# LayerNorm's scaling of 48 tiles on GpSimd in place of ScalarE, in a fused cross-attention kernel

## The chip, the cores and the metric

The kernel runs on one core of one Trainium2 chip. A core has a matrix engine (TensorE, PE in the profile, with PEld for its weight loads), a vector engine (VectorE, DVE), a scalar engine (ScalarE, ACT), GpSimd (POOL), and SyncE (SP), which here only issues DMAs. Each engine executes its own instructions in the order in which the program lists them, and waits for other engines by semaphores. The metric is device time in microseconds (us) of one execution.

## The reference

The layer is cross-attention with a residual and a LayerNorm: x is (4, 2048, 512), the context is (4, 77, 512), there are 16 heads of 32 columns, and a mask hides part of the 77 context rows.

```python
qs  = (q @ wq) ; ks_ = (k @ wk) ; vs = (v @ wv)          # split into 16 heads of 32
scores = einsum('bhqd,bhkd->bhqk', qs, ks_) / sqrt(32)
scores = where(mask, -inf, scores)
attn = einsum('bhqk,bhkd->bhqd', softmax(scores), vs)     # heads joined again
out  = attn @ wo + q
mu   = mean(out) ; var = mean((out - mu) ** 2)            # over the 512 columns
return (out - mu) / sqrt(var + 1e-5) * gamma + beta
```

The change concerns the last line alone.

## The kernel before, in words

The 8192 rows of x are cut into 64 tiles of 128 rows. Two tiles make a pair (32 pairs), four tiles share one transposed load of x. Every product that needs it is split into a high part and a low remainder, so three matmuls stand for one.

The whole order of the work is written out by hand in a table of words, ORDER (lines 49 to 143). The kernel walks through it and calls one small function per word; since each engine executes in program order, the table sets the order on every engine. A word is a letter and a number, which is a tile, a pair or a group. The words that matter here:

- Q (PE) and q (DVE): the query projection, and its copy out of PSUM. i (ACT, line 265) and j (POOL, line 269): the high part and the remainder of the transposed x, 128x1024 each.
- S (PE, line 399): the scores of a tile. T (DVE, line 416): mask added and row maxima, four heads at a time. e (ACT, line 431): the exponentials, four heads at a time, with their sums. r (DVE, line 441): reciprocals of the sums. n (POOL, line 446): the tile's weights times these reciprocals, 128x1232.
- t (DVE, line 467): transpose of the weights. P (issued by SP mostly, line 478): twelve DMAs per pair that regroup them. V (PE, line 492): product with the values. a (ACT, line 521) and b (DVE, line 525): high part and remainder of its result.
- x (SP, line 533): a tile of x is loaded as the residual. O (PE, line 548): the output projection. + (DVE, line 557): the residual is added, which gives the tile o, 128x512.
- s (DVE, lines 568 and 569): mean and variance of the tile. v (POOL, lines 574 to 577): once per pair, the inverse root of variance plus epsilon, and minus the mean times that root. k (ACT, line 583): the tile times the root, plus the shift, in one pass over 128x512. f (POOL, lines 587 and 588): times gamma, then plus beta. w (SP, line 591): the tile is stored.

Tiles 48 to 63 go another way (letters u, y and z: DVE does the passes) and contain none of k, f and v. The tile o has eight buffers, the pair's mean and variance (mv) and its root (rn) three each. SP issues all loads, stores and most of the regrouping DMAs from one queue, in the table's order.

Of the kernel before, what the change touches and what calls it, by code (L numbers as in the profile page):

```python
# [8 lines left out]
F32 = mybir.dt.float32  # L9
# [3 lines left out]
AF = mybir.ActivationFunctionType  # L13
ALU = mybir.AluOpType
# [3 lines left out]
P = 128  # L18
# [31 lines left out]
R1 R0 R3 E l0 l2 C2 C0 C1 C3 g5 M4.4 A0 M0.1 M12.4 A1 M1.3 A3 M8.4 K2 A2 H2 J3 p i3 g4 J1 K0 i2 S0 I2 j2 S1 T0.1  # L50
e0.1 T0.2 H0 T0.0 j3 e0.0 T1.0 T0.3 e0.2 T1.1 Q4 T1.2 e0.3 F0 T1.3 I0 e1.2 r0 n0 S2 q4 e1.0 S3 T2.3 T2.0 Q7 i5 T2.1
e1.3 F2 j5 T2.2 t0 e1.1 Q6 i4 F1 g7 r1 Y1 e2.0 F3 L1 n1 T3.2 Q5 x1 T3.1 e2.1 q6 T3.3 e3.3 j4 t1 B0 e3.2 T3.0 P0.4s
q7 x2 e2.3 q5 P0.7s S4 D0 P0.5s e3.0 S6 P0.10s T4.3 P0.0s G0 B2 e3.1 R2 T4.0 g6 P0.2s e4.3 r3 P0.8s G3 n3 P0.11s B1
e2.2 D2 P0.6s T4.1 T4.2 e4.1 G2 r2 Q8 i7 t3 x11 n2 P0.3s e4.2 P0.9s T6.0 P0.1s T6.2 e4.0 j7 x0 Q9 T6.3 Z13.s t2
e6.0 Z0.s G1 e6.3 S5 r4 P1.0s T6.1 n4 P1.7s q8 Q10 e6.2 T5.3 P1.6s T5.0 P1.10s e6.1 T5.2 P1.3s T5.1 P1.5s i6 S7 t4
P1.1s Z1.s e5.3 Q11 j6 P1.11s T7.2 P1.9s e7.2 T7.3 Z2.s q9 P1.8s r6 e7.3 D1 Q13 n6 P1.4s T7.0 P1.2s T7.1 e7.0 g9
q10 x3 e7.1 Z12.s V0 q13 g8 q11 Z11.s a0.0 r7 e5.0 t6 V1 Z10.s n7 Z7.s e5.1 b0.0 S9 N t7 a1.1 Q12 e5.2 b1.1 P3.9s
a1.0 P3.5s r5 T9.0 n5 P3.11s e9.0 Q14 b1.0 P3.3s T9.2 Z8.s e9.2 T9.1 P3.2s T9.3 P3.4s e9.3 t5 Y0 S8 P3.10s a0.1 O2
P3.7s q12 i9 T8.1 P3.0s T8.0 e9.1 P2.3s T8.3 P3.8s q14 Z9.s e8.0 O3 T8.2 P3.1s b0.1 P3.6s e8.3 +2 Z5.s r9 P2.0s n9
e8.2 S10 +3 P2.7s S11 P2.2s T10.0 e8.1 s2 P2.9s O1 j9 s3 T10.3 e10.3 r8 T10.1 v1 g10 Q15 +1 e10.1 Z4.s t9 n8 P2.6s  # L60
k2 x6 T10.2 P2.11s e10.0 V3 f2 t8 i8 T11.3 P4.11s O0 e11.3 T11.2 P2.4s j8 q15 P4.9s a3.0 T11.0 P2.8s k3 T11.1 P2.1s
a3.1 S12 w2 e10.2 M16.4 P2.5s b3.1 Q19 +0 P4.6s e11.1 r10 P4.5s T12.2 n10 P2.10s b3.0 e11.2 T12.0 P4.10s O6 s0
P4.7s i10 f3 P4.8s s1 P4.0s e11.0 q19 T12.3 S13 e12.2 t10 v0 w3 V2 P4.3s r11 x7 T13.2 a2.0 n11 e13.2 P4.1s T13.1 O7
Z6.s +6 P4.4s T12.1 a2.1 k1 b2.0 P4.2s b2.1 e12.0 Z3.s f1 t11 O4 x4 x5 e12.3 g11 s6 P5.5s e12.1 j10 T13.3 P5.0s O5
# [20 lines left out]
P12.5s k18 S28 +20 P12.9s i17 V11 T28.1 g18 e28.1 T28.2 P12.10s j17 T28.0 P12.11s S29 s20 e28.2 P12.0s P12.6s t26
Q33 v10 P12.4s a11.1 e27.1 P12.2s f18 b11.1 P12.3s T29.0 a11.0 T28.3 Q32 e28.3 P12.8s r27 T29.2 x24 n27 b11.0 e28.0
T29.1 q33 O23 k20 T29.3 e29.0 M32.4 q32 r28 t27 k21 O22 i18 f21 +23 P13.10s e29.3 s23 x27 w18 e29.2 S30 +22 n28 w21
P13.5s V12 T30.1 e30.1 P13.9s T30.0 P13.6s T30.2 j18 a12.0 S31 x26 s22 e30.2 P13.2s T30.3 Q34 P13.3s t28 e29.1
P13.1s v11 P13.4s a12.1 T31.0 P13.7s f20 e30.3 T31.3 Q35 P13.11s T31.2 g19 e31.3 r29 P13.8s b12.1 P13.0s b12.0 n29
k23 q34 O25 T31.1 e30.0 f23 t29 e31.2 O24 +25 e31.0 P14.4s s25 x29 w20 k22 r30 q35 n30 P14.2s i19 S32 g20 +24  # L90
P14.7s V13 T32.1 e32.1 P14.10s j19 T32.2 P14.9s T32.0 e32.2 w23 S33 s24 P14.11s t30 Q37 P14.3s a13.1 v12 e31.1 x28
P14.5s T32.3 f22 b13.1 a13.0 P14.6s e32.3 T33.0 Q36 P14.1s r31 T33.2 P14.8s e32.0 q37 n31 P14.0s b13.0 x31 T33.1
e33.0 O27 T33.3 M36.4 k25 t31 k24 f25 e33.3 O26 q36 P15.1s r32 P15.6s +27 i20 w22 s27 n32 w25 e33.2 P15.10s S34 +26
e33.1 V14 x30 T34.1 j20 P15.11s T34.0 a14.0 P15.2s T34.2 e34.1 S35 P15.4s s26 P15.8s t32 Q38 v13 e34.2 P15.5s g21
# [10 lines left out]
t39 k32 f33 O34 i24 +35 s35 e41.3 q44 n40 w33 e41.2 P19.10s S42 +34 P19.5s V18 T42.1 e42.1 P19.9s j24 T42.0 x38
T42.2 P19.2s a18.0 S43 s34 e42.2 P19.3s t40 P19.6s Q46 v17 e41.1 P19.8s P19.1s T42.3 f32 P19.4s T43.0 a18.1 e42.3
P19.7s T43.3 Q47 P19.0s T43.2 e43.3 g25 r41 b18.1 n41 P19.11s b18.0 x41 q46 k35 O37 T43.1 e42.0 f35 t41 e43.2 q47
P20.7s O36 r42 w32 +37 e43.0 n42 P20.1s s37 L3 k34 w35 i25 P20.5s S44 +36 P20.9s j25 V19 T44.1 e44.1 P20.10s T44.2
P20.11s T44.0 P20.4s e44.2 S45 s36 P20.6s t42 g26 Q49 v18 a19.1 P20.8s e43.1 P20.2s f34 b19.1 P20.3s T45.0 a19.0
# [64 lines left out]
def xattn_layernorm(  # L174
# [404 lines left out]
    def scale(t):  # L579
        o = od[t]  # L580
        tt = t % 2
        rn = rns[t // 2]
        nc.scalar.activation(o, o, AF.Identity, bias=rn[:, 1, tt : tt + 1], scale=rn[:, 0, tt : tt + 1])  # L583
# [176 lines left out]
```

## Time and profile before

| What | Value |
|---|---|
| median of 3 runs | 526.71 us (525.96 to 527.35) |
| span of the profiled execution, first to last instruction | 525.7 us |
| PE busy | 507.2 us, 96% |
| DVE busy | 476.0 us, 91% |
| ACT busy | 460.4 us, 88% |
| POOL busy | 405.5 us, 77% |
| k on ACT (line 583) | 48 passes, 37.9 us busy, 807 ns each |
| f on POOL (lines 587, 588) | 48 and 48 passes, 62.5 and 62.4 us busy, 1302 and 1300 ns each |
| n on POOL (line 446) | 63 whole tiles, 142.8 us busy, 2267 ns each |
| granted PE clock | 0.997 of full speed |

The profiled execution's own time beside its span is not listed apart: the profile gives the span alone, and the three runs give times of whole executions, whose median lies 1.0 us above it.

A busy share is an average over the span. The chain of waits follows the last instruction back, at each step to what released it or to the instruction before it on its engine. A group's row gives busy time, the mean duration of one, the engine's idle time just before, and who ended that idle time.

### The profile page before, as it was taken

How to read it: one execution, taken by the hardware profiler on the slowest of the kernel's cores; microseconds unless marked ns; L12 is line 12 of the kernel's file. 1: busy time of each engine (PE TensorE's matmuls, PEld its weight loads, DVE VectorE, ACT ScalarE, POOL GpSimd, SP SyncE). 2: the span in 40 equal slices, each digit the busy share in tenths (PEclk: the TensorE clock that was granted, in tenths of full speed). 3: DMA queues.
4: the chain of work that ended last, by engine and by line, in shares of the span. 5: the costliest groups of instructions: out<-in, count | busy, mean ns of one | idle time of the engine just before them, and what ended most of it. 6: DMA issues, size and time to landing. Idle time of an engine off the chain costs nothing.

```text
span 525.7 us, 20274 instructions
## 1 busy us (share of the span) xinstructions
PE 507.2 (96%) x6845; PEld 388.8 (74%) x6845; DVE 476.0 (91%) x2572; ACT 460.4 (88%) x2215; POOL 405.5 (77%) x371
## 2 busy tenths in 40 slices
PE   9999999999989999999999999999999999999994
PEld 6987777778767777777777777767777777767662
DVE  5798988989979989998989989998998999999997
ACT  6699999998989999999999999999999999987400
POOL 2475736889889889969989887988888689869551
PEclk9999999999999999999999999999999999999998
DMA  8948577785797677988887687797868987388555
GB/s 300 401 125 241 148 205 196 195 236 147 205 243 226 189 197 225 217 219 219 215 225 207 178 224 226 184 254 195 213 190 225 259 251 189 91 219 218 158 176 199
DMA packets 59261, 110.85 MB, mean 211 GB/s; under 512 B 9430, under 2 KB 11758, under 8 KB 59158
## 3 DMA queue, kind: packets, MB, share of 16 engines
q1 hardware_dynamic: 55702, 102.75, 69.1%
q0 software_dynamic: 2496, 5.77, 3.9%
q10 hardware_dynamic: 960, 1.05, 0.8%
q8 instruction: 54, 0.88, 0.7%
q14 instruction: 49, 0.40, 0.3%
HBM read 41.79 MB, written 16.78 MB: 111 GB/s over the span
## 4 chain that ended last, share of the span: by engine, by line
PE 51%; DVE 12%; DMA 10%; POOL 9%; SPq 9%; ACT 5%; issue 3%; POOLq 0%; DVEq 0%
PE pq L275 20%; PE po L548 15%; PE sc L399 7%; SPq L478 6%; PE pa L492 6%; DMA PT<-B 6%; ACT pbuf L431 4%; POOL o L587 3%; DVE B L467 3%; POOL o L588 2%; POOL pbuf L446 2%; DVE pbuf L416 2%; PE pv L326 2%; DMA stage_a<-xT 1%; POOL xtl L269 1%
## 5 line engine op out<-in xcount | busy, mean ns | idle before, releaser
L431 ACT ACTIVATE pbuf<-pbuf,nm 128x77 f32<-128x77 f32 x1024 | 352.7, 350 | 16.2 <-DVE nm L416 13.4
L431 ACT ACTIVATION_READ_ACCUMULATOR pbuf<-pbuf,nm 128x1 f32 x1024 | 194.6, 190 | 0.0
L416 DVE CUSTOM_DVE_ANT_0 pbuf<-sc,mb 128x77 f32<-128x77 f32 x1024 | 170.2, 231 | 9.6 <-PE sc L399 8.5
L446 POOL TENSOR_TENSOR pbuf<-pbuf,ri 128x1232 f32<-128x1232 f32 x63 | 142.8, 2267 | 39.4 <-DVE ri L441 23.6
L467 DVE STREAM_TRANSPOSE B<-pbuf 128x1280 f32<-128x1280 f32 x64 | 96.1, 1502 | 9.8 <-POOL pbuf L446 5.4
L548 PE MATMUL po<-woh,AH 128*128 128x512 f32 x256 | 102.6, 401 | 0.0
L548 PE MATMUL po<-woh,AL 128*128 128x512 f32 x256 | 100.1, 391 | 2.3 <-DVE AL L525 2.3
L275 PE MATMUL pq<-xth,wqh 128*128 128x512 f32 (+1 forms) x256 | 101.8, 398 | 0.2
L548 PE MATMUL po<-wol,AH 128*128 128x512 f32 x256 | 99.8, 390 | 0.0
L275 PE MATMUL pq<-xtl,wqh 128*128 128x512 f32 (+1 forms) x256 | 98.3, 384 | 0.0
L275 PE MATMUL pq<-xth,wql 128*128 128x512 f32 (+1 forms) x256 | 98.1, 383 | 0.0
L416 DVE DVE_READ_ACCUMULATOR2_ANT nm<- 128x1 f32 x1024 | 83.9, 82 | 0.0
L399 PEld LDWEIGHTS sc<-kct,q 32*64 32x64 f32 x4096 | 52.8, 130 | 32.9 <-issue 17.1
L587 POOL TENSOR_TENSOR o<-o,gam 128x512 f32<-128x512 f32 x48 | 62.5, 1302 | 13.7 <-ACT o L583 13.4
L269 POOL TENSOR_TENSOR xtl<-xtf,xth 128x1024 fp32r<-128x1024 f32 x28 | 67.3, 2403 | 6.7 <-ACT xth L265 6.6
L399 PE MATMUL sc<-kct,q 32*64 32x77 f32 x4096 | 63.6, 238 | 8.4 <-issue 3.8
L588 POOL TENSOR_TENSOR o<-o,bet 128x512 f32<-128x512 f32 x48 | 62.4, 1300 | 3.8
L492 PE MATMUL pa<-PT,vsb 96*32 96x256 f32 x992 | 59.9, 382 | 0.0
L521 ACT CAST AH<-pa 128x512 fp32r<-128x512 f32 x64 | 36.4, 572 | 25.0 <-DVE st L596 10.6
L548 PEld LDWEIGHTS po<-woh,AL 128*128 128x128 f32 x256 | 48.0, 188 | 13.8 <-DVE AL L525 3.5
L548 PEld LDWEIGHTS po<-woh,AH 128*128 128x128 f32 x256 | 48.0, 188 | 13.7 <-issue 2.0
L275 PEld LDWEIGHTS pq<-xth,wqh 128*128 128x128 f32 x256 | 48.1, 188 | 12.0 <-PE sc L399 0.5
(108 smaller groups left out, 666.0 us busy)
## 6 DMA issues: line engine op xcount, KB each, us to landing
PT<-B SPq DMA_DIRECT2D x343, 128.0 KB
xtf<-xT SPq DMA_DIRECT2D x28, 512.0 KB
o<-x SPq DMA_DIRECT2D x56, 256.0 KB
out<-o SPq DMA_DIRECT2D x56, 256.0 KB
PT<-B POOLq DMA_DIRECT2D x25, 128.0 KB, 3.8
xtf<-xT SPq DMA_DIRECT2D x4, 256.0 KB
stage_a<-wq SPq DMA_DIRECT2D x4, 256.0 KB
stage_a<-wk SPq DMA_DIRECT2D x4, 256.0 KB
```

The lines of the kernel that those rows point to most:

```text
L269: nc.gpsimd.tensor_tensor(l[:, c : c + 2], fx.pop((g, c)), xh[g][:, c : c + 2].bitcast(F32), ALU.subtract)
L275: nc.tensor.matmul(pq, w[:, c, m * P : (m + 1) * P], r[g][:, c, rs], start=(n == 0), stop=(n == 11))
L399: mm = nc.tensor.matmul(sc[j][r0 : r0 + SR, g * NK : (g + 1) * NK], qs[q, g, rs.start + r0 : rs.start + r0 + SR], kct[q, g, t // TPB, keys ...
L416: nc.vector.tensor_tensor_reduce(pb[:, h // 2, (h % 2) * NK : (h % 2 + 1) * NK], scs[t][j][:, g * NK : (g + 1) * NK], mb[:, t % TPB, keys_ ...
L431: nc.scalar.activation(pb[:, h // 2, (h % 2) * NK : (h % 2 + 1) * NK], pb[:, h // 2, (h % 2) * NK : (h % 2 + 1) * NK], AF.Exp, bias=nmax[t ...
L446: nc.gpsimd.tensor_tensor(pv, pv, rv.to_broadcast((P, NP, 2, NK)), ALU.mult)
L467: nc.vector.transpose(bt.rearrange("p c q r -> p q c r"), pbuf[t % NPB].rearrange("p q (c r) -> p q c r", c=5),)
L492: nc.tensor.matmul(pas[b, g // 2][HD * j : HD * (j + 1), (g % 2) * BLK : (g % 2 + 1) * BLK], vsb[:, 2 * b // TPB, h % 2, HD * (h // 2) : H ...
L521: nc.scalar.copy(*at_part(once(ahs, b, [P, NG, BLK], F32R, "AH"), b, i, by_tile))
L548: nc.tensor.matmul(pos[t], a[:, c, rs], w[:, c, :], start=(first and c == 0 and n == 0), stop=(c == NC_D - 1 and n == 2),)
L587: nc.gpsimd.tensor_tensor(o, o, gam, ALU.mult)
L588: nc.gpsimd.tensor_tensor(o, o, bet, ALU.add)
```

## The change

The words k0 to k47 are taken out of ORDER; the other words keep their order. What k did becomes the first of three passes in f: POOL subtracts the mean and multiplies by the root in one tensor_scalar instruction over 128x512, in place, with the two numbers of each row read from mv and rn. Since the mean is used as it is, v no longer makes the product of mean and root and its negative, and keeps two of its four operations on 128x2.

```diff
     def rsqrt(b):
-        rn = rns[b] = buf([P, 2, 2], F32, "rn", name=f"rn_{b}")
-        mv = mvs[b]
-        nc.gpsimd.tensor_tensor(rn[:, 0, :], mv[:, :, 1], eps, ALU.add)
-        nc.gpsimd.tensor_tensor(rn[:, 0, :], rn[:, 0, :], mhalf, ALU.pow)
-        nc.gpsimd.tensor_tensor(rn[:, 1, :], mv[:, :, 0], rn[:, 0, :], ALU.mult)
-        nc.gpsimd.tensor_tensor(rn[:, 1, :], rn[:, 1, :], mneg, ALU.mult)
-
-    def scale(t):
-        o = od[t]
-        tt = t % 2
-        rn = rns[t // 2]
-        nc.scalar.activation(o, o, AF.Identity, bias=rn[:, 1, tt : tt + 1], scale=rn[:, 0, tt : tt + 1])
+        rn = rns[b] = buf([P, 2], F32, "rn", name=f"rn_{b}")
+        nc.gpsimd.tensor_tensor(rn, mvs[b][:, :, 1], eps, ALU.add)
+        nc.gpsimd.tensor_tensor(rn, rn, mhalf, ALU.pow)
 
     def affine(t):
-        o = od[t]
+        o, tt = od[t], t % 2
+        mean, rstd = mvs[t // 2][:, tt, 0:1], rns[t // 2][:, tt : tt + 1]
+        nc.gpsimd.tensor_scalar(o, o, mean, rstd, ALU.subtract, ALU.mult)
         nc.gpsimd.tensor_tensor(o, o, gam, ALU.mult)
         nc.gpsimd.tensor_tensor(o, o, bet, ALU.add)
...
-        "v": lambda k, part: rsqrt(k), "k": lambda k, part: scale(k), "f": lambda k, part: affine(k),
+        "v": lambda k, part: rsqrt(k), "f": lambda k, part: affine(k),
```

The order of POOL's instructions in the middle of the program, before, from the split of x for group 9 to the normalise of tile 30 (o_20 and o_23 are tiles of the output, rn_11 the roots of pair 11, ri_29 the reciprocals of tile 29; the last figure of each name only numbers the buffers):

```order
L269 TENSOR_TENSOR xtl_9_4324<-xtf_9_0_4037,xth_9_4224 128x1024
L574 TENSOR_TENSOR rn_11_4399<-mv_11_4237,small_78 128x2
L575 TENSOR_TENSOR rn_11_4399<-rn_11_4399,small_78 128x2
L576 TENSOR_TENSOR rn_11_4399<-mv_11_4237,rn_11_4399 128x2
L577 TENSOR_TENSOR rn_11_4399<-rn_11_4399,small_78 128x2
L587 TENSOR_TENSOR o_20_3657<-o_20_3657,gam_76 128x512
L588 TENSOR_TENSOR o_20_3657<-o_20_3657,bet_77 128x512
L446 TENSOR_TENSOR pbuf2_82<-pbuf2_82,ri_29_4447 128x8x154
L587 TENSOR_TENSOR o_23_3617<-o_23_3617,gam_76 128x512
L588 TENSOR_TENSOR o_23_3617<-o_23_3617,bet_77 128x512
L446 TENSOR_TENSOR pbuf0_80<-pbuf0_80,ri_30_4513 128x8x154
```

The same place on POOL now (line numbers have shifted: 442 is the normalise, 575 the new pass):

```order
L265 TENSOR_TENSOR xtl_9_4301<-xtf_9_0_4016,xth_9_4200 128x1024
L569 TENSOR_TENSOR rn_11_4376<-mv_11_4214,small_78 128x2
L570 TENSOR_TENSOR rn_11_4376<-rn_11_4376,small_78 128x2
L575 TENSOR_SCALAR o_20_3639<-o_20_3639,mv_10_3943,rn_10_4094 128x512
L576 TENSOR_TENSOR o_20_3639<-o_20_3639,gam_76 128x512
L577 TENSOR_TENSOR o_20_3639<-o_20_3639,bet_77 128x512
L442 TENSOR_TENSOR pbuf2_82<-pbuf2_82,ri_29_4423 128x8x154
L575 TENSOR_SCALAR o_23_3599<-o_23_3599,mv_11_4214,rn_11_4376 128x512
L576 TENSOR_TENSOR o_23_3599<-o_23_3599,gam_76 128x512
L577 TENSOR_TENSOR o_23_3599<-o_23_3599,bet_77 128x512
L442 TENSOR_TENSOR pbuf0_80<-pbuf0_80,ri_30_4488 128x8x154
```

Two small operations on rn have gone, and a pass over 128x512 stands ahead of each multiplication by gamma, between two normalises.

The order of ACT's instructions around the scaling of tiles 20 and 21, before (line 431 are exponentials, x8 means eight in a row, line 583 is the scaling, line 265 the high part of x):

```order
L431 ACTIVATE pbuf1_81,sum_28_4039<-pbuf1_81,nm_28_4032 128x77 x8
L583 ACTIVATE o_20_3657<-o_20_3657,rn_10_4115 128x512
L431 ACTIVATE pbuf2_82,sum_29_4199<-pbuf2_82,nm_29_4133 128x77 x4
L583 ACTIVATE o_21_3409<-o_21_3409,rn_10_4115 128x512
L265 CAST xth_9_4224<-xtf_9_0_4037 128x1024
L431 ACTIVATE pbuf2_82,sum_29_4199<-pbuf2_82,nm_29_4133 128x77 x8
```

And now:

```order
L427 ACTIVATE pbuf1_81,sum_28_4018<-pbuf1_81,nm_28_4011 128x77 x8
L427 ACTIVATE pbuf2_82,sum_29_4176<-pbuf2_82,nm_29_4111 128x77 x4
L261 CAST xth_9_4200<-xtf_9_0_4016 128x1024
L427 ACTIVATE pbuf2_82,sum_29_4176<-pbuf2_82,nm_29_4111 128x77 x8
L427 ACTIVATE pbuf0_80,sum_30_4286<-pbuf0_80,nm_30_4281 128x77 x4
```

The two scalings between the exponentials have gone; all else on ACT stands as it stood.

More of the change, by code (lines that the diff above doesn't have):

```diff
@@ L55 @@
[L55 to L64, printed above, removed]
@@ L85 @@
[L85 to L94, printed above, removed]
@@ L105 @@
[L105 to L109, printed above, removed]
@@ new lines @@
+t25 e26.0 f19 q31 P12.7s e27.2 O20 r26 w16 +21 P12.1s s21 e27.0 n26 w19 L2 P12.5s S28 +20 P12.9s i17 V11 T28.1 g18
+e28.1 T28.2 P12.10s j17 T28.0 P12.11s S29 s20 e28.2 P12.0s P12.6s t26 Q33 v10 P12.4s a11.1 e27.1 P12.2s f18 b11.1
+P12.3s T29.0 a11.0 T28.3 Q32 e28.3 P12.8s r27 T29.2 x24 n27 b11.0 e28.0 T29.1 q33 O23 T29.3 e29.0 M32.4 q32 r28 t27
+O22 i18 f21 +23 P13.10s e29.3 s23 x27 w18 e29.2 S30 +22 n28 w21 P13.5s V12 T30.1 e30.1 P13.9s T30.0 P13.6s T30.2 j18
+a12.0 S31 x26 s22 e30.2 P13.2s T30.3 Q34 P13.3s t28 e29.1 P13.1s v11 P13.4s a12.1 T31.0 P13.7s f20 e30.3 T31.3 Q35
@@ new lines @@
+Q58 e52.1 T52.3 g31 r51 P24.2s T53.3 n51 e52.2 x62 T53.1 x60 Q57 q58 P24.6s e53.1 b23.0 P24.4s t51 w43 e52.3 T53.2 S54
+P25.4s a23.1 T53.0 P25.1s Q59 T54.2 P25.9s e54.2 T54.1 g30 b23.1 e53.0 r52 T54.3 P25.0s n52 Q56 T54.0 w42 e54.3 s44
+x55 P25.10s q57 v22 e53.2 P25.2s t52 P25.8s S55 P25.3g e53.3 P25.7s M56.4 V24 T55.3 e54.0 T55.2 M60.4 P25.6s O47 r53
+T55.0 a24.0 n53 i31 q56 P25.11s b24.0 P25.5s e54.1 q59 x59 T55.1 j31 S56 i30 t53 X49 a24.1 r54 P26.0s O46 T56.2
+P26.10g e55.3 P26.11s b24.1 n54 +47 x51 T56.3 e55.2 P26.9s T56.0 P26.3s O49 P26.4g +46 x48 e55.1 j30 t54 P26.1s e55.0
```

143 lines of the change are left out of this document (77 added, 66 removed).

## The prediction, made before the changed kernel was run

> **What bounds the kernel now.** I read the page's busy shares first, then the chain of waits, then the groups and waits of GpSimd (POOL), whose queue takes the new work.
>
> ```profile
> PE 507.2 (96%) x6845; PEld 388.8 (74%) x6845; DVE 476.0 (91%) x2572; ACT 460.4 (88%) x2215; POOL 405.5 (77%) x371
> ...
> PE 51%; DVE 12%; DMA 10%; POOL 9%; SPq 9%; ACT 5%; issue 3%; POOLq 0%; DVEq 0%
> ```
>
> PE is busy nearly throughout, yet holds only half of the chain that ended last; the rest passes through every other engine. No engine bounds the span alone. POOL's 77% is an average over stages: the scaling that moves runs between the first rsqrt (v) and the last, so I look there.
>
> ```profile
> L574 POOL TENSOR_TENSOR rn<-mv,small x24: 189/196/208, 87.2 to 441.9; 128x2 f32<-128x2 f32 x24
> ...
> 87.00:442.00 355.00, 347.73 (x4830) 267.49 (x4829) 324.40 (x1846) 337.33 (x1620) 306.76 (x260) 1.00 0.78 213
> ```
>
> The first row (the instructions that touch rn) gives the pace: 24 v's, one per pair of tiles, from 87.2 to 441.9 us, so a pair takes (441.9 - 87.2) / 23 = 15.42 us. The second (busy time by engine in that stretch, in the order PE, PEld, DVE, ACT, POOL) shows POOL at 306.8 of 355 us, 86%, and ACT at 337.3, 95%. One pair on POOL, from its timeline (start, duration):
>
> ```profile
> 243.32 0.19 POOL L574 TENSOR_TENSOR rn<-mv,small 128x2 f32<-128x2 f32 x1
> 243.59 0.70 POOL L575 TENSOR_TENSOR rn<-rn,small 128x2 f32<-128x2 f32 x1
> 244.37 0.20 POOL L576 TENSOR_TENSOR rn<-mv,rn 128x2 f32<-128x2 f32 x1
> 244.64 0.20 POOL L577 TENSOR_TENSOR rn<-rn,small 128x2 f32<-128x2 f32 x1
> 244.79 1.30 POOL L587 TENSOR_TENSOR o<-o,gam 128x512 f32<-128x512 f32 x1
> 246.17 1.30 POOL L588 TENSOR_TENSOR o<-o,bet 128x512 f32<-128x512 f32 x1
> 247.42 2.26 POOL L446 TENSOR_TENSOR pbuf<-pbuf,ri 128x1232 f32<-128x1232 f32 x1
> 249.64 1.30 POOL L587 TENSOR_TENSOR o<-o,gam 128x512 f32<-128x512 f32 x1
> 251.01 1.29 POOL L588 TENSOR_TENSOR o<-o,bet 128x512 f32<-128x512 f32 x1
> 252.96 2.25 POOL L446 TENSOR_TENSOR pbuf<-pbuf,ri 128x1232 f32<-128x1232 f32 x1 [0.66 <-DVE ri L441]
> 255.18 2.36 POOL L269 TENSOR_TENSOR xtl<-xtf,xth 128x1024 fp32r<-128x1024 f32 x1
> 257.50 0.19 POOL L574 TENSOR_TENSOR rn<-mv,small 128x2 f32<-128x2 f32 x1
> ```
>
> From v to v 14.18 us, with 0.66 us of waiting: POOL's own work is 13.5 us per pair. At a mean of 15.42 it has 1.9 us per pair to spare.
>
> **The change, part by part.** Removed: 48 ACT passes (k), and two of the four small operations of each v. Added: 48 POOL passes at the head of f. Nothing else changes place: k issues no DMA, and SP, PE and DVE keep their order.
>
> *The price of the new pass.* No row shows a POOL tensor_scalar, so I bound it from these groups (busy us, mean ns | idle before, released by):
>
> ```profile
> L446 POOL TENSOR_TENSOR pbuf<-pbuf,ri 128x1232 f32<-128x1232 f32 x63 | 142.8, 2267 | 39.4 <-DVE ri L441 23.6 <-DMA PT<-B 7.9 <-DVE nm L416 7.0
> L458 POOL TENSOR_TENSOR pbuf<-pbuf,ri 128x616 f32<-128x616 f32 x2 | 2.8, 1392 | 3.3 <-DVE ri L452 3.2
> L269 POOL TENSOR_TENSOR xtl<-xtf,xth 128x1024 fp32r<-128x1024 f32 x28 | 67.3, 2403 | 6.7 <-ACT xth L265 6.6
> L587 POOL TENSOR_TENSOR o<-o,gam 128x512 f32<-128x512 f32 x48 | 62.5, 1302 | 13.7 <-ACT o L583 13.4
> L318 POOL MEMSET vsb<- 32x1024 f32 x3 | 2.8, 944 | 0.1
> L583 ACT ACTIVATE o<-o,rn 128x512 f32<-128x512 f32 x48 | 37.9, 807 | 0.0
> ```
>
> Two full operands cost (2403 - 1302) / 512 = 2.15 ns per element over a fixed 1302 - 512 x 2.15 = 201 ns. One full operand and one repeated 77 times (L446 against L458) costs (2267 - 1392) / 616 = 1.42 ns per element. Only writing costs at most 944 / 1024 = 0.92. The new pass reads one full operand and two numbers per row, so 512 elements cost at least 0.47 us (the memset's rate), at most about 1.30 us (L587, as if both numbers were streams), and by its nearest row, L446, 512 x 1.42 + 201 = 0.93 us. I take 0.9, since its constants change less often than L446's. With the 0.07 us that POOL leaves between two dependent passes (249.64 + 1.30 to 251.01) the step is 0.97 us.
>
> [...]
>
> *Per pair.* v loses 244.79 - 244.37 = 0.42 us, two f's gain 2 x 0.97: 13.5 + 1.5 = 15.0 of 15.42 us. POOL stays a little below the pace, with 0.4 us of slack where it had 1.9. The mean is now read by f instead of v; its tile has three buffers, one per pair, and f follows its v within about a pair (20's f stands behind v 11 in the order shown above), so DVE's next writer of that buffer, two pairs later, has no cause to wait. If POOL fell two pairs behind it would, and DVE's maxima behind it.
>
> *What lies on the path.* The chain of waits passes through 11 of the 48 f's. Seven are entered from POOL's or SP's own earlier work, so each pays the whole step:
>
> ```profile
> 112.40 1.26 POOL o L587
> 125.86 1.26 POOL o L587
> 128.48 1.26 POOL o L587
> 131.09 1.26 POOL o L587
> ...
> 334.60 0.21 POOL rn L576
> 334.87 0.20 POOL rn L577
> 335.07 1.26 POOL o L587
> 339.92 1.26 POOL o L587
> ...
> 371.09 1.27 POOL o L587
> ```
>
> That is 7 x 0.97 = +6.8 us, less 0.4 us for the one v there. The other four are entered from ACT, whose late pass had left POOL idle:
>
> ```profile
> 107.37 1.29 POOL L587 TENSOR_TENSOR o<-o,gam 128x512 f32<-128x512 f32 x1 [0.98 <-ACT o L583]
> 326.38 1.30 POOL L587 TENSOR_TENSOR o<-o,gam 128x512 f32<-128x512 f32 x1 [1.70 <-ACT o L583]
> 356.08 1.30 POOL L587 TENSOR_TENSOR o<-o,gam 128x512 f32<-128x512 f32 x1 [1.69 <-ACT o L583]
> 387.07 1.30 POOL L587 TENSOR_TENSOR o<-o,gam 128x512 f32<-128x512 f32 x1 [1.67 <-ACT o L583]
> ```
>
> There the new pass starts at once and fills the gap: 0.97 less 0.98, 1.70, 1.69 and 1.67, together -2.2 us if nothing else is late. The next normalise needs its reciprocals too, so I take half, -1.1. For the 37 f's off the chain, whose slack shrinks to 0.4 us per pair, I add one more pass, +1.0: what is queued behind each f on POOL is the normalise, and DVE's transpose, the regrouping DMAs and PE's values' product wait for that.
>
> *SP's queue.* SP issues stores and regroupings in one order, so a later f also holds regroupings back. The waits of SP, and the chain where it shows:
>
> ```profile
> SPq L591 <- POOL o L588: 28.9, 17, 4.5
> ...
> 134.12 1.46 SPq L591
> ```
>
> 17 stores already wait for f. This is how the steps at 125.86 to 131.09 reach the end; it is in the seven.
>
> *ACT.* It gives up 48 x 0.807 = 38.7 us, 1.6 per pair. I cost that at nothing beyond the -1.1: ACT is 5% of the chain, and POOL and PE follow at once.
>
> Sum: 6.8 - 0.4 - 1.1 + 1.0 = +6.3 us on a span of 525.7, 532.0. The median of the runs shown, 526.71, lies 1.0 above that span, so the forecast is 533.0 us.
>
> **The rivals.**
>
> *POOL becomes the bound outright.* With the pass at 1.30 us the step is 1.37 and a pair 13.5 + 2.74 - 0.42 = 15.8 us, above 15.42: 23 pairs x 0.4 = +9 us if POOL never waits, and with a quarter of today's 1.9 us of waiting still there, 23 x 0.9 = +20 us, 547. I put the case at 526.7 + 16 = 543. It decides from a pass of about 1.1 us. For it: the pass makes two operations per element, L446 one. Against: L446's rate.
>
> *No change.* With the pass near 0.55 us the step is 0.62: seven make +4.3, v -0.4, the four gaps -3.6 in full, sum +0.3: 527.0. For it: memset's rate, and POOL's 13.4 us of waits for ACT that vanish. Against: every POOL row that reads SBUF is dearer.
>
> *Faster, through ACT.* At 95% of the stretch ACT may be the hidden bound: the exponentials behind each k come 0.7 us sooner, the reciprocals too, and the 23.6 us that the normalise (L446) waits for them shrink. At 0.47 us per pass the seven cost 3.8, v and the gaps return 4.3, and a tenth of the 23.6 goes: -2.9, 523.8. It decides below 0.5 us per pass. Against: the chain holds ACT for 5%.
>
> **How the numbers follow.** Forecast case (pass 0.6 to 1.1 us): 0.52, its own range 529 to 538. POOL outright: 0.20. No change: 0.21. Faster: 0.07. The predicted time is the likeliest case's, 533.0. The range runs from 527.0, the no-change price, to 545, inside the POOL case; it leaves out the faster case and the upper tail. A measurement here tells about 0.3%, 1.6 us, from no change, so: faster 0.07, same 0.20, slower 0.73.
>
> **What would show it.** The new pass in its own group on POOL with a mean of 0.9 us (0.6 to 1.1); POOL's wait for ACT at the head of f gone; POOL busy about 340 us in the stretch from first to last v; that stretch about 6 us longer, and the part behind it unchanged; ACT at some 300 us in it with new idle time; SP's waits for f up from 28.9 us. Wrong would be: a mean below 0.55 or above 1.2 us, the pace per pair shorter than 15.42 us, or the time lost in the tail from 442 us on.

## The result: 588.05 us, slower by 11.7%

| | before | after |
|---|---|---|
| median | 526.34 us (4 runs, 523.75 to 527.35) | 588.05 us (4 runs, 586.67 to 591.57) |
| ratio after / before | | 1.117, 95% interval 1.113 to 1.122 |
| span of the profiled execution | 525.7 us | 586.2 us |
| POOL busy, first to last v | 306.8 of 355 us | 392.0 of 412 us |
| pace, one pair of tiles | 15.42 us | 17.90 us |

The prediction said 533.0 us, 527 to 545; the time lies 43 us above that range. The profiled executions of e1 and e4 below (557.69 and 548.87 us) ran more than 1.5% longer than the fastest of the same kernel, and only the durations of single POOL passes are taken from them.

### The profile page after: what moved, and what is told of

Its sections match the earlier page's. It is cut to its first block, busy times and chain, and to the rows that moved or that the text cites. A ratio compares the mean times of both kernels' runs of the same rounds, so it can differ in the third digit from the quotient of the medians.

```text
span 586.2 us, 20195 instructions
## 1 busy us (share of the span) xinstructions
PE 530.4 (90%) x6845; PEld 397.3 (68%) x6845; DVE 477.7 (81%) x2572; ACT 428.7 (73%) x2167; POOL 496.9 (85%) x371
## 3 DMA queue, kind: packets, MB, share of 16 engines
q10 hardware_dynamic: 960, 1.05, 0.7%
## 4 chain that ended last, share of the span: by engine, by line
POOL 57%; PE 16%; DVE 14%; DMA 5%; SPq 5%; issue 3%; POOLq 0%; ACTq 0%; ACT 0%; DVEq 0%
POOL pbuf L442 16%; POOL o L575 13%; POOL o L577 9%; POOL o L576 8%; POOL xtl L265 8%; PE pq L271 6%; SPq L474 4%; DVE B L463 4%; PE po L544 3%; DVE pbuf L412 3%; POOL rn L570 2%; PE sc L395 2%; PE pa L488 2%; PE pk L294 1%; PE pq L644 1%
## 5 line engine op out<-in xcount | busy, mean ns | idle before, releaser
L442 POOL TENSOR_TENSOR pbuf<-pbuf,ri 128x1232 f32<-128x1232 f32 x63 | 142.8, 2267 | 36.6 <-DVE ri L437 27.2
L271 PE MATMUL pq<-xth,wqh 128*128 128x512 f32 (+1 forms) x256 | 104.5, 408 | 12.7 <-DVE nm L412 6.3
L271 PE MATMUL pq<-xtl,wqh 128*128 128x512 f32 (+1 forms) x256 | 100.9, 394 | 6.1 <-POOL xtl L265 6.1
L575 POOL TENSOR_SCALAR o<-o,mv,rn 128x512 f32<-128x512 f32 x48 | 100.3, 2089 | 0.1
L271 PE MATMUL pq<-xth,wql 128*128 128x512 f32 (+1 forms) x256 | 99.7, 389 | 0.0
L395 PE MATMUL sc<-kct,q 32*64 32x77 f32 x4096 | 72.8, 242 | 23.4 <-DVE nm L412 6.1
L395 PEld LDWEIGHTS sc<-kct,q 32*64 32x64 f32 x4096 | 58.4, 133 | 52.3 <-issue 27.0
L488 PE MATMUL pa<-PT,vsb 96*32 96x256 f32 x992 | 63.7, 398 | 1.0 <-DMA vsb<-v 0.6
L271 PEld LDWEIGHTS pq<-xtl,wqh 128*128 128x128 f32 x256 | 49.4, 193 | 18.1 <-POOL xtl L265 9.4
```

The costliest lines, as they stand in the source:

```text
L271: nc.tensor.matmul(pq, w[:, c, m * P : (m + 1) * P], r[g][:, c, rs], start=(n == 0), stop=(n == 11))
L395: mm = nc.tensor.matmul(sc[j][r0 : r0 + SR, g * NK : (g + 1) * NK], qs[q, g, rs.start + r0 : rs.start + r0 + SR], kct[q, g, t // TPB, keys ...
L442: nc.gpsimd.tensor_tensor(pv, pv, rv.to_broadcast((P, NP, 2, NK)), ALU.mult)
L488: nc.tensor.matmul(pas[b, g // 2][HD * j : HD * (j + 1), (g % 2) * BLK : (g % 2 + 1) * BLK], vsb[:, 2 * b // TPB, h % 2, HD * (h // 2) : H ...
L575: nc.gpsimd.tensor_scalar(o, o, mean, rstd, ALU.subtract, ALU.mult)
```

## The profile after

The busy shares, four rows of the 40 slices (in tenths, left to right through the span; PEclk is the clock that PE was granted), and the shares of the chain of waits, by engine and then by line:

```profile
PE 530.4 (90%) x6845; PEld 397.3 (68%) x6845; DVE 477.7 (81%) x2572; ACT 428.7 (73%) x2167; POOL 496.9 (85%) x371
...
PE   9999999987799989899898998989898799999984
...
POOL 3466548999999999999999999999999949979751
PEclk9999999999799979999999999979999989999998
...
POOL 57%; PE 16%; DVE 14%; DMA 5%; SPq 5%; issue 3%; POOLq 0%; ACTq 0%; ACT 0%; DVEq 0%
POOL pbuf L442 16%; POOL o L575 13%; POOL o L577 9%; POOL o L576 8%; POOL xtl L265 8%; PE pq L271 6%; SPq L474 4%; DVE B L463 4%; PE po L544 3%; DVE pbuf L412 3%; POOL rn L570 2%; PE sc L395 2%; PE pa L488 2%; PE pk L294 1%; PE pq L644 1%
```

Before, POOL held 9% of the chain (the path of waits followed back from the last instruction) and PE 51%. Now POOL holds 57%, and its row shows nines without a gap from the eighth slice to the thirty-second (103 to 469 us). The 85% beside its name again hides that, because the head and the tail are averaged in.

The groups of POOL by line (busy us, mean ns | idle time before them and who ended it):

```profile
L442 POOL TENSOR_TENSOR pbuf<-pbuf,ri 128x1232 f32<-128x1232 f32 x63 | 142.8, 2267 | 36.6 <-DVE ri L437 27.2 <-DVE nm L412 6.0 <-DMA PT<-B 3.4
L575 POOL TENSOR_SCALAR o<-o,mv,rn 128x512 f32<-128x512 f32 x48 | 100.3, 2089 | 0.1
L265 POOL TENSOR_TENSOR xtl<-xtf,xth 128x1024 fp32r<-128x1024 f32 x28 | 67.5, 2412 | 1.9 <-ACT xth L261 1.9
L577 POOL TENSOR_TENSOR o<-o,bet 128x512 f32<-128x512 f32 x48 | 62.9, 1310 | 3.8
L576 POOL TENSOR_TENSOR o<-o,gam 128x512 f32<-128x512 f32 x48 | 61.7, 1286 | 4.0
```

The new pass (L575) takes 2089 ns, not 900. It is dearer than the two passes behind it, each of which reads two full operands, and nearly as dear as the normalise, which has 2.4 times its elements. Nothing makes it wait: its idle time is 0.1 us over 48 passes. The other groups kept their price (2267, 2403, 1302 and 1300 ns before).

The row of the v's, among the instructions that touch rn (durations, first and last start):

```profile
L569 POOL TENSOR_TENSOR rn<-mv,small x24: 182/195/323, 88.1 to 499.7; 128x2 f32<-128x2 f32 x24
```

The stretch between them (its length, busy time of PE, PEld, DVE, ACT and POOL, then PE's clock, the DMA share and GB/s):

```profile
88.00:500.00 412.00, 371.03 (x4838) 277.04 (x4836) 326.08 (x1844) 308.72 (x1581) 391.98 (x260) 0.97 0.67 184
```

One pair from POOL's timeline (start, duration):

```profile
269.55 0.19 POOL L569 TENSOR_TENSOR rn<-mv,small 128x2 f32<-128x2 f32 x1
269.81 0.71 POOL L570 TENSOR_TENSOR rn<-rn,small 128x2 f32<-128x2 f32 x1
270.51 2.08 POOL L575 TENSOR_SCALAR o<-o,mv,rn 128x512 f32<-128x512 f32 x1
272.68 1.29 POOL L576 TENSOR_TENSOR o<-o,gam 128x512 f32<-128x512 f32 x1
274.05 1.29 POOL L577 TENSOR_TENSOR o<-o,bet 128x512 f32<-128x512 f32 x1
275.30 2.25 POOL L442 TENSOR_TENSOR pbuf<-pbuf,ri 128x1232 f32<-128x1232 f32 x1
277.54 2.07 POOL L575 TENSOR_SCALAR o<-o,mv,rn 128x512 f32<-128x512 f32 x1
279.69 1.27 POOL L576 TENSOR_TENSOR o<-o,gam 128x512 f32<-128x512 f32 x1
281.04 1.27 POOL L577 TENSOR_TENSOR o<-o,bet 128x512 f32<-128x512 f32 x1
282.27 2.25 POOL L442 TENSOR_TENSOR pbuf<-pbuf,ri 128x1232 f32<-128x1232 f32 x1
284.49 2.38 POOL L265 TENSOR_TENSOR xtl<-xtf,xth 128x1024 fp32r<-128x1024 f32 x1
286.83 0.19 POOL L569 TENSOR_TENSOR rn<-mv,small 128x2 f32<-128x2 f32 x1
```

From v to v it is 17.28 us without one wait. The prediction's own load per pair, 13.5 - 0.42 + 2 x (pass + 0.07), gives 17.4 us at a pass of 2.09. The measured pace is (499.7 - 88.1) / 23 = 17.90 us.

The half microsecond between load and pace is not waited in every pair. Between 103 and 467 us POOL waits 0.2 us in all, and the 16 steps from the fifth v (147.41 us) to the twenty-first (426.01 us) take 17.41 us on average, the load itself. The waits lie at the ends of the stretch: 1.65 us at its beginning and these two behind 467 us (in brackets the idle time before the instruction and what ended it):

```profile
472.84 2.25 POOL L442 TENSOR_TENSOR pbuf<-pbuf,ri 128x1232 f32<-128x1232 f32 x1 [4.97 <-DVE nm L412]
480.30 2.25 POOL L442 TENSOR_TENSOR pbuf<-pbuf,ri 128x1232 f32<-128x1232 f32 x1 [3.43 <-DMA PT<-B]
```

So the time went here: 23 x (17.90 - 15.42) = 57.0 us between the first and the last v. The rest of the 60.5 us between the spans is 0.9 ahead of the first v (88.1 against 87.2) and 2.7 behind the last (586.2 - 499.7 = 86.5 against 525.7 - 441.9 = 83.8).

Who waits for POOL now is seen in the waits of DVE, ACT and SP's queue (us in total, times, longest):

```profile
DVE B L463 <- POOL pbuf L442: 74.0, 25, 6.9
...
ACT pbuf L427 <- DVE nm L412: 83.1, 37, 7.1
...
SPq L474 <- DVE B L463: 66.7, 23, 5.9
SPq L580 <- POOL o L577: 65.5, 17, 8.1
```

Before, these were 5.4 us (DVE's transpose for the normalise), 13.4 (the exponentials for the maxima), 33.7 and 28.9 us. The normalise comes late, the transpose behind it holds up DVE's maxima, and ACT, which gave up 38 us of work, waits 70 us longer for those. POOL's 13.4 us of waiting for ACT at the head of f are gone, as forecast, and gained nothing.

## The experiments

The theory after the result: POOL sets the pace, through the price of one instruction. The rivals: the price belongs to the two row scalars or to the operation count; the loss has a part that comes from ACT's freed time or from PE's clock; the rest of the prediction's sum was wrong as well.

### What the new pass pays for

Half the columns (the other half is not scaled):

```diff
-        nc.gpsimd.tensor_scalar(o, o, mean, rstd, ALU.subtract, ALU.mult)
+        nc.gpsimd.tensor_scalar(o[:, :256], o[:, :256], mean, rstd, ALU.subtract, ALU.mult)
```

> The new pass covers only the first 256 of 512 columns; columns 256 to 511 are left unscaled. Theory 1 (GpSimd's own load sets the pace, and the pass has a price per element): from 2.09 us per pass, with the 0.20 us fixed part of the other GpSimd passes, 0.20 + 1.89/2 = 1.15 us per pass; a pair on GpSimd is then 13.1 + 2 x (1.15 + 0.07) = 15.5 us instead of 17.4, and with the 0.5 us of waiting per pair that the changed kernel shows, the time falls by 23 x 1.9 = 43 us to about 545 us. Rival (the price is per instruction, from reading the two numbers of each row): the mean stays near 2 us and the time near 588. Rival (the lower granted PE clock, 0.977, sets the time): clock and time stay where they are.

One operation in place of two (the mean is subtracted, the root left out):

```diff
-        nc.gpsimd.tensor_scalar(o, o, mean, rstd, ALU.subtract, ALU.mult)
+        nc.gpsimd.tensor_scalar(o, o, mean, None, ALU.subtract)
```

> The new pass subtracts the mean and leaves the multiplication by the root out. If the price is per arithmetic operation, the mean falls from 2.09 us to about 0.20 + 1.89/2 = 1.15 us and the time to about 545 us. If GpSimd runs the same loop for one operation as for two, it stays at 2.0 to 2.1 us and the time at about 588 us.

Two constants in place of the two numbers per row (the tile is not normalised):

```diff
-        nc.gpsimd.tensor_scalar(o, o, mean, rstd, ALU.subtract, ALU.mult)
+        nc.gpsimd.tensor_scalar(o, o, 0.125, 1.5, ALU.subtract, ALU.mult)
```

> The new pass does the same two operations with constants (minus 0.125, times 1.5) in place of the row's mean and root, so the scaling itself is left out. If the price comes from the two numbers read per row, the mean falls below 1.3 us and the time to 550 us or less. If it comes from the loop over elements, the mean stays at 2.0 to 2.1 us and the time at about 588 us.

One pass with two operands, the second a number per row that is repeated along the columns (the mean is left out):

```diff
-        nc.gpsimd.tensor_scalar(o, o, mean, rstd, ALU.subtract, ALU.mult)
+        nc.gpsimd.tensor_tensor(o, o, rstd.to_broadcast((P, D)), ALU.mult)
```

> The new pass is one tensor_tensor that multiplies by the root, broadcast along the row; the mean is not subtracted. It has the shape of the normalise, whose rate gives 512 x 1.42 + 201 ns = 0.93 us. If the prediction's sum was right and only its price wrong, this kernel comes out where the forecast stood: GpSimd at 13.1 + 2 x 1.0 = 15.1 us per pair, the time 6 us above before, 529 to 538 us. If GpSimd's queue loses more than the sum says (long passes in front of the normalise hurt whatever they cost), it is above 545 us.

The whole computation in two such passes:

```diff
-        nc.gpsimd.tensor_scalar(o, o, mean, rstd, ALU.subtract, ALU.mult)
+        nc.gpsimd.tensor_tensor(o, o, mean.to_broadcast((P, D)), ALU.subtract)
+        nc.gpsimd.tensor_tensor(o, o, rstd.to_broadcast((P, D)), ALU.mult)
```

> The changed kernel with the pass written as two: the mean subtracted, then the root multiplied, each as a two-operand pass whose second operand is one number per row, repeated. At 1.06 us each and 0.07 between, the step is 2.19 instead of 2.16 us: load 17.5 us per pair, pace 18.0, 588 to 592 us. If the repeated operand had been cheaper than the row's numbers of the one-pass form: below 583 us.

The groups of the new pass by line. Of e1, 256 columns:

```profile
L575 POOL TENSOR_SCALAR o<-o,mv,rn 128x256 f32<-128x256 f32 x48 | 60.1, 1253 | 0.1
```

Of e2, one operation:

```profile
L575 POOL TENSOR_SCALAR o<-o,mv 128x512 f32<-128x512 f32 x48 | 75.7, 1577 | 0.1
```

Of e3, constants:

```profile
L575 POOL TENSOR_SCALAR o<-o 128x512 f32<-128x512 f32 x48 | 92.7, 1931 | 0.1
```

Of e4, one two-operand pass:

```profile
L575 POOL TENSOR_TENSOR o<-o,rn 128x512 f32<-128x512 f32 x48 | 51.0, 1062 | 0.0
```

Of e11, two of them:

```profile
L576 POOL TENSOR_TENSOR o<-o,rn 128x512 f32<-128x512 f32 x48 | 50.3, 1049 | 3.8
L575 POOL TENSOR_TENSOR o<-o,mv 128x512 f32<-128x512 f32 x48 | 50.1, 1044 | 0.0
```

| kernel | pass, us | time, us | ratio to before, with its interval |
|---|---|---|---|
| after | 2.09 | 588.05 | 1.117 (1.113 to 1.122) |
| e1, 256 columns | 1.25 | 545.78 | one execution, no interval |
| e2, one operation | 1.58 | 566.15 | 1.069 (1.063 to 1.076) |
| e3, constants | 1.93 | 580.74 | 1.097 (1.090 to 1.104) |
| e4, one two-operand pass | 1.06 | 543.13 | 1.026 (1.019 to 1.033) |
| e11, two of them | 1.04 + 1.05 | 591.04 | 1.121 (1.114 to 1.128) |

- The price grows with the elements: (2089 - 1253) / 256 = 3.27 ns per element, over 1253 - 256 x 3.27 = 416 ns fixed. The pass was expected at 1.15 us and the time at 545; the rival, a price per instruction, falls.
- The second operation, with its number per row, costs 2089 - 1577 = 512 ns, 1.0 ns per element; with one operation an element still costs (1577 - 416) / 512 = 2.27 ns, if the fixed part is the same. So one operation came out between the two values that were expected.
- Both row scalars together cost 2089 - 1931 = 158 ns. As the main part of the price they fall out.
- A two-operand pass with a repeated second operand does one such operation in 1.06 us, half a microsecond less than e2. The whole computation in two of them costs the same 2.09 us as the one instruction, plus one more step of 0.07, and e11's time is as expected, 588 to 592. Fusing the two operations into one instruction saved only that step.

### What else the 60 us contain

The pass left out (tiles 0 to 47 are not normalised), which is the change without its price:

```diff
-        nc.gpsimd.tensor_scalar(o, o, mean, rstd, ALU.subtract, ALU.mult)
```

> The scaling pass is left out altogether: tiles 0 to 47 are multiplied by gamma and get beta, but are not normalised, so the output is not the layer's. v has its two operations, ACT has lost its 48 passes, as in the changed kernel. This is the change without its price. My reading (before, ACT's passes cost only the four places of the chain where POOL waited for ACT, 0.98 to 1.70 us each, of which I took half): 523 to 527 us. Rival (ACT was a hidden bound, and the change would have paid with a cheap pass): the 37.9 us of passes were worth a quarter or more, so 517 us or less. POOL's load should be 13.1 us per pair and the pace 15.3 to 15.4 us.

Measured: 528.9 us beside 528.0 of before, ratio 1.000 (0.997 to 1.004). ACT's freed 38 us are worth nothing that can be told, though the stretch between the v's shows that they are free. The row of its v's:

```profile
L569 POOL TENSOR_TENSOR rn<-mv,small x24: 187/195/207, 87.3 to 441.0; 128x2 f32<-128x2 f32 x24
```

The stretch from 87 to 441 us, columns as above:

```profile
87.00:441.00 354.00, 349.76 (x4831) 268.90 (x4830) 327.04 (x1847) 306.40 (x1574) 298.26 (x214) 1.00 0.77 214
```

ACT is busy 306 us in place of 337 and POOL 298 in place of 307, and the pace is (441.0 - 87.3) / 23 = 15.38 us against 15.42. PE is at 349.8 of 354 us. The expected 1 to 5 us of gain were not there: what the prediction hoped for from the four gaps that ACT left on the chain did not show. In this order of the work even a free pass would not have paid.

ACT's passes put back as copies, beside the new pass on POOL (k stands at its old places):

```diff
+    def scale(t):
+        o = od[t]
+        nc.scalar.activation(o, o, AF.Identity, bias=0.0, scale=1.0)
...
-        "v": lambda k, part: rsqrt(k), "f": lambda k, part: affine(k),
+        "v": lambda k, part: rsqrt(k), "k": lambda k, part: scale(k), "f": lambda k, part: affine(k),
```

> The changed kernel, and the 48 ACT passes stay where they stood, as copies with scale 1 and bias 0. If the 60 us come from POOL alone, ACT's 38 us fit into its idle time (308.7 us busy of 412): 585 to 592 us, the same as the changed kernel. Rival (the loss is held down by what ACT gained, or ACT's late exponentials pace the tiles): up to 38 us longer, 600 us or more.

Measured: 588.07 us (587.37 to 588.59), where the changed kernel has 588.05. ACT's work costs nothing that can be told, with the new pass (e6) or without it (e5).

v with its four operations again (the last two write numbers that nothing reads):

```diff
-        rn = rns[b] = buf([P, 2], F32, "rn", name=f"rn_{b}")
-        nc.gpsimd.tensor_tensor(rn, mvs[b][:, :, 1], eps, ALU.add)
-        nc.gpsimd.tensor_tensor(rn, rn, mhalf, ALU.pow)
+        rn = buf([P, 2, 2], F32, "rn", name=f"rn_{b}")
+        rns[b] = rn[:, 0, :]
+        mv = mvs[b]
+        nc.gpsimd.tensor_tensor(rn[:, 0, :], mv[:, :, 1], eps, ALU.add)
+        nc.gpsimd.tensor_tensor(rn[:, 0, :], rn[:, 0, :], mhalf, ALU.pow)
+        nc.gpsimd.tensor_tensor(rn[:, 1, :], mv[:, :, 0], rn[:, 0, :], ALU.mult)
+        nc.gpsimd.tensor_tensor(rn[:, 1, :], rn[:, 1, :], mneg, ALU.mult)
```

> The changed kernel, with v's two removed operations put back (the mean times the root, and its negative, which nothing reads). If POOL sets the pace, 0.42 us per v for 23 paces is +9.7 us: 595 to 600 us, and the pace goes from 17.9 to 18.3 us. Rival (something else sets the pace and POOL is only near it): 586 to 591 us.

Measured: 597.61 us (597.32 to 599.42), +9.6 over the changed kernel where +9.7 was expected. The v's of its profile:

```profile
L571 POOL TENSOR_TENSOR rn<-mv,small x24: 185/198/325, 87.2 to 508.4; 128x2 f32<-128x2 f32 x24
```

The pace is (508.4 - 87.2) / 23 = 18.31 us, 0.41 more. Each 0.42 us on POOL's queue comes back whole: POOL sets the pace, and shortening v was worth 9.6 us here.

More work for PE, as a test of its clock (two matmuls whose product is overwritten, at each query projection from group 1 on and each output projection):

```diff
+FILL = 2
...
+        for _ in range(FILL if g else 0):
+            nc.tensor.matmul(pq, wqh[:, 0, :P], wqh[:, 1, :], start=True, stop=True)
...
+            for _ in range(FILL):
+                nc.tensor.matmul(pos[t], wqh[:, 0, :P], wqh[:, 1, :], start=True, stop=True)
```

> The changed kernel, with two more matmuls (their product is overwritten) ahead of each query projection from group 1 on and of each output projection, about 1.8 us of PE per pair, so that PE idles less and its granted clock should stay at 0.99 or above where the changed kernel shows 0.977. If POOL sets the pace, PE's half-clock stretches cost nothing there, and PE has room (16.1 of 17.9 us per pair): 584 to 591 us, clock or no clock. Rival (the half-clock stretches are part of the 60 us: lost clock of about 13 us): 573 to 580 us. If PE becomes the bound instead: above 595 us.

The reason for it, in the changed kernel: three pairs of neighbouring stretches of time (columns: length, PE busy, its granted clock, DMA share, GB/s):

```profile
142.70:146.10 3.40, 0.80 (x4) 1.00 0.19 44
146.10:152.90 6.80, 3.27 (x8) 0.51 0.95 257
...
275.80:279.20 3.40, 1.74 (x8) 1.00 0.51 154
279.20:282.60 3.40, 2.06 (x84) 1.00 0.47 115
...
381.60:385.00 3.40, 1.75 (x69) 1.00 0.57 181
385.00:391.80 6.80, 6.80 (x107) 0.51 0.76 230
```

In the first pair and the last, a stretch of 3.4 us in which PE works 0.80 or 1.75 us is followed by 6.8 us at half clock. In the second it works 1.74 us and the clock stays, so PE's busy time in such a stretch alone does not tell when the clock falls. Before, the mean granted clock was 0.997 and is now 0.977.

Measured: 593.49 us (593.15 to 594.47) at a mean clock of 0.988 to 0.993, so neither 584 to 591 nor 573 to 580. The v's and their stretch say where the 5.4 us are. The v's:

```profile
L574 POOL TENSOR_TENSOR rn<-mv,small x24: 186/197/316, 91.5 to 504.6; 128x2 f32<-128x2 f32 x24
```

The stretch from 92 to 505 us:

```profile
92.00:505.00 413.00, 398.26 (x5019) 306.61 (x5018) 326.35 (x1846) 309.04 (x1583) 392.19 (x258) 0.99 0.67 183
```

The first v comes 3.4 us later (91.5 against 88.1), since the head has extra matmuls on a busy PE. From there the pace is (504.6 - 91.5) / 23 = 17.96 us against 17.90, with PE busy 27 us longer and the clock at 0.99 in place of 0.97. Giving PE its clock back gained nothing in that stretch. By itself this leaves open whether the added matmuls hid a small gain. The trace of the changed kernel closes that for the middle: about 20 us of half clock lie between 103 and 467 us (three stretches of 6.8 us, from 146.2, 211.1 and 385.2 us), and POOL, whose work fills the pace there, waited 0.2 us in all. The expectation missed what the matmuls cost in the head.

### Whether the rest of the sum was right

The first test was e4, whose edit stands above: with the sum right and only the price wrong, 529 to 538 us was expected, with POOL's queue losing more than the sum says, above 545. Measured: 543.13 us (540.35 to 546.41), so neither. With e4's pass the prediction's sum is 7 x (1.062 + 0.07) - 0.4 - 1.1 + 1.0 = +7.4 us; its interval says +10.0 to +17.5 on the 528.48 us beside it. At a load of 15.3 us per pair, just below the pace of 15.4, the sum is too low.

A pass at the price that the prediction took (400 columns times the root; the other 112 are not scaled and no mean is subtracted):

```diff
-        nc.gpsimd.tensor_scalar(o, o, mean, rstd, ALU.subtract, ALU.mult)
+        nc.gpsimd.tensor_tensor(o[:, :400], o[:, :400], rstd.to_broadcast((P, 400)), ALU.mult)
```

> The pass is one multiply by the root, repeated over the first 400 columns; the other 112 columns are not scaled and no mean is subtracted. At the 1.42 ns per element of the 1.06 us pass over 512 columns it should take about 0.90 us: the price that the prediction took. If the rest of the prediction's sum was right (+6.3 us on the runs beside it), 532 to 536 us. Rival (with POOL near the pace, short waits of PE bring its granted clock down, which the sum left out; the 512-column pass came out at 545 us at a clock of 0.98): 538 to 546 us, and shorter in the runs with the higher clock.

The group of the pass by line:

```profile
L575 POOL TENSOR_TENSOR o<-o,rn 128x400 f32<-128x400 f32 x48 | 42.1, 877 | 0.0
```

The row of the v's:

```profile
L569 POOL TENSOR_TENSOR rn<-mv,small x24: 188/197/225, 88.4 to 446.4; 128x2 f32<-128x2 f32 x24
```

Measured: a pass of 0.88 us, 536.14 us (535.38 to 536.52), ratio 1.017 (1.012 to 1.021), at a clock of 0.991 to 0.996. That is +6.4 to +11.3 us by the interval. The prediction's sum for such a pass is 7 x (0.877 + 0.07) - 0.4 - 1.1 + 1.0 = +6.1, just below that interval, and +7.2 inside it without the -1.1 for ACT's gaps, for which e5 shows no gain. The time lies 0.1 us above the first theory's 532 to 536 us and below the rival's 538 to 546, and the clock did not fall. The pace is (446.4 - 88.4) / 23 = 15.57 us.

The change on half of the tiles (odd pairs on POOL, even pairs on ACT as before):

```diff
+        o, tt = od[t], t % 2
+        if t // 2 % 2:
+            mean, rstd = mvs[t // 2][:, tt, 0:1], rns[t // 2][:, 0, tt : tt + 1]
+            nc.gpsimd.tensor_scalar(o, o, mean, rstd, ALU.subtract, ALU.mult)
```

> The kernel before, with the scaling moved to POOL for the odd pairs alone (24 tiles); the even pairs keep ACT's pass and all four operations of v. POOL's load is 13.5 us for an even pair and 17.4 for an odd one, 15.45 on average, which is the pace of before, 15.4. If POOL's order needs the 0.5 us over its load that the dearer variants show, pace 15.95: 23 x 0.5 = +12 us, about 540 us. Rival (the odd pairs' excess of 2 us is not caught up in the even ones, since what POOL delays is waited for at once): 23 x 1.2, 555 us. If buffers even it out: below 533 us.

Measured: 553.33 us, ratio 1.050 (1.044 to 1.057). The number is the rival's, its reason is not. The timeline shows that the order mostly spreads the passes by itself, so that few pairs are heavy or light: in 13 of the 23 steps one f with the pass and one without stand between two v's.

```profile
254.18 0.20 POOL L574 TENSOR_TENSOR rn<-mv,small 128x2 f32<-128x2 f32 x1
...
255.13 1.29 POOL L592 TENSOR_TENSOR o<-o,gam 128x512 f32<-128x512 f32 x1
...
260.05 2.09 POOL L591 TENSOR_SCALAR o<-o,mv,rn 128x512 f32<-128x512 f32 x1
...
269.39 0.19 POOL L574 TENSOR_TENSOR rn<-mv,small 128x2 f32<-128x2 f32 x1
```

The row of its v's:

```profile
L574 POOL TENSOR_TENSOR rn<-mv,small x24: 186/197/210, 88.0 to 467.9; 128x2 f32<-128x2 f32 x24
```

This pair takes 15.21 us, yet the pace over all is (467.9 - 88.0) / 23 = 16.52 us. Where the load equals the pace of before, waiting adds 1.1 us per pair. Unlike in the changed kernel the waits are many and short: between the first v and the last, POOL waits 7.0 us for reciprocals (9 times), 7.0 for maxima (3 times, one of them 5.0) and 4.8 for the mean (5 times). The step behind the one shown, 269.39 to 289.43 us, takes 20.0 us, and the mean granted clock of this execution is 0.978, where before has 0.997. Whether the clock or the mutual waiting makes the 1.1 is open.

One matmul more per projection beside the pass over 256 columns, FILL = 1 in the edit of e8 (columns 256 to 511 are not scaled), to see whether PE's clock costs time where POOL is only near the pace:

> The pass over the first 256 columns alone (the other 256 are not scaled), with one more matmul, whose product is overwritten, ahead of each query projection from group 1 on and of each output projection, about 0.9 us of PE per pair. The same pass without the matmuls gave 545.8 us at a granted clock of 0.993 and 557.7 us at 0.973. If the half-clock stretches of PE are what cost those 12 us, more work on PE keeps the clock at 0.99 or above and all executions lie at 545 to 550 us (1.7 us of that are the matmuls in the head). Rival (the clock falls where something else holds the tiles up, and costs little by itself): some executions still take 555 us or more, at a clock above 0.985 too. If PE, at 16.0 of about 16.3 us per pair, becomes the bound: above 552 us in all of them, with PE busy over 97% between the first and the last v.

Measured: 551.19 us (549.98 to 552.34) at a clock of 0.994 to 0.999. That is 1 us above the first theory's range, below the rival's 555, and below the 552 us of the third in three executions of four. In its stretch PE is almost full, which a clean test would have had to avoid. Its v's:

```profile
L574 POOL TENSOR_TENSOR rn<-mv,small x24: 184/194/209, 89.5 to 464.2; 128x2 f32<-128x2 f32 x24
```

The stretch from 88 to 472 us:

```profile
88.00:472.00 384.00, 377.91 (x5108) 291.89 (x5108) 338.92 (x1912) 314.74 (x1621) 362.01 (x270) 1.00 0.75 201
```

PE is at 98% (377.9 of 384 us), and the time is 5.4 us above e1's 545.78, 1 to 2 of them in the head (89.5 against 87.0 to 88.4 us in the kernels without the matmuls). What half clock costs near the pace is not settled by this run.

The paces of the kernels together, without e1 and e4 (e6 has 17.90 and e8 17.96 us at the load of after). The load per pair is 13.1 us plus the passes with 0.07 us for each, and 0.4 more for e7; for e10 it is the mean over even and odd pairs:

| kernel | load, us | pace, us | pace less load |
|---|---|---|---|
| e5, no pass | 13.1 | 15.38 | 2.3 |
| e9, 0.88 us | 15.0 | 15.57 | 0.6 |
| e10, half of the tiles | 15.45 | 16.52 | 1.1 |
| e12, 1.25 us and more work on PE | 15.7 | 16.29 | 0.6 |
| e2, 1.58 us | 16.4 | 16.96 | 0.6 |
| e3, 1.93 us | 17.1 | 17.59 | 0.5 |
| after, 2.09 us | 17.4 | 17.90 | 0.5 |
| e11, 1.04 + 1.05 us | 17.6 | 17.96 | 0.4 |
| e7, 2.09 us and long v | 17.8 | 18.31 | 0.5 |

Without a pass the pace is that of the others' work, 15.4 us. From a load of 16.4 us on it is POOL's load and, on average, half a microsecond, which the changed kernel spends at the ends of the stretch.

## Why the prediction was wrong, point by point

- **The price of the new pass** is the step that failed. 0.9 us was taken, with 1.30 as the upper bound; it is 2.09. The bound rested on the belief that a number per row can cost at most as much as a full operand. L587 reads two streams for one operation, and the new pass is another kind of instruction, with two operations. The prediction named the two operations, but only as an argument for a rival. No row of before showed this kind, and the same subtraction takes 1.58 us in e2 and 1.04 in the first pass of e11, so the kind counts and not the operands alone. The nearest row, L446, was a good indication of a repeated operand in a two-operand pass (0.93 forecast, 1.06 measured), which is not what the kernel runs. With the bound wrong, the range was wrong too.
- **The rival "POOL becomes the bound outright"** was the right one, at 0.20, and its arithmetic held once the price is put right. It gave a pair 13.5 - 0.42 plus two steps, left a quarter of 1.9 us of waiting, and put the deciding point at about 1.1 us. With the measured price it gives 13.5 - 0.42 + 4.32 + 0.5 = 17.9 us, and 17.90 was measured; 23 x 2.48 = +57 us. That the 0.5 fits is luck: it stood for waiting left in every pair, and the trace has it in a few long waits at the ends.
- **The chain's sum** (seven steps, half of four gaps, one pass for the rest) was +6.1 at the price that e9 has, against +6.4 to +11.3 measured, and +7.4 at e4's, against +10.0 to +17.5. It is a little low at a load of 15.0 us and clearly low at 15.3, inside the forecast's own range of prices; beside the 60 us it is a small part. What it leaves out there is open.
- **ACT's relief** was taken at half of 2.2 us, and the rival "faster, through ACT" had 0.07. e5 and e6 measured nothing for it, with the pass and without.
- **v** at -0.42 us per pair was right in size. The prediction used it once, on the chain; with POOL as the bound it counts in all 23 pairs, 9.6 us in e7.
- **SP's queue** did what was said, and more: the waits of the stores for f rose from 28.9 to 65.5 us, those of the regroupings for the transpose from 33.7 to 66.7.
- Of the signs named in advance: POOL's wait for ACT at the head of f is gone (right); the tail grew by 2.7 us, and e5, which has no pass at all, has a tail of 528.0 - 441.0 = 87.0 us too, so that is not the pass; ACT is at 309 us in the stretch with new idle time (right); POOL is at 392 us there, not 340; the stretch is 57 us longer, not 6; and the mean of the group is above 1.2, the sign that was said to refute the forecast.

## What to carry to other kernels

An instruction whose kind does not occur in the trace has no upper bound from rows of other kinds: count its operations as well as the operands it reads (here the bound was 1.30 us, and the pass took 1.58 us with one operation and 2.09 with two), and write down what the time would be at twice the price. Before work moves to an engine, compare that engine's own work per step of the pipeline, taken from its timeline, with the pace. Here a load of 15.0 us under a pace of 15.4 cost 1.7% and one of 15.3 already 2.6%; beyond the pace every nanosecond counted at every step. And ask what the relieved engine's time is worth at all: here 38 us less on an engine that was busy 95% of the stretch bought nothing, while PE was busy 98% of it.

## What the runs showed of the hardware

- On GpSimd a tensor_scalar over 128x512 in float32 takes 2.09 us with two operations and a number per row for each, 1.93 with constants, 1.58 with one operation, and 1.25 over 256 columns. A tensor_tensor whose second operand is one number per row repeated takes 1.06 us (1.04 to 1.05 in e11, and 0.88 over 400 columns, so 1.5 to 1.65 ns per element), less than the 1.30 us with two full operands.
- In the changed kernel PE's granted clock fell to half for 6.8 us after stretches of 3.4 us in which PE worked 0.80 and 1.75 us, and did not fall after one with 1.74. Where POOL set the pace this cost no time that shows: POOL waited 0.2 us in the 364 us that hold three such drops, and in e8 the pace stays within 0.06 us whether the clock is 0.97 or 0.99.
